# Ten gate buffers and an earlier, regrouped issue of a step's transfers in a fused window-attention and mixture-of-experts kernel

## Chip, cores and metric

The kernel runs on one core of one Trainium2 chip. The metric is the device time of one execution in microseconds (us), from the first to the last instruction and what the launch adds around them; a lower number is better. The figure for the kernel before is the median of 3 runs.

## What is computed

The input `x` is a float32 image of shape (2, 128, 256, 256): 2 images, 128 channels, 256 by 256 pixels. The layer does two things, one after the other, each with a residual addition:

```python
x = x + conv_ref(_ln_c(x), W_qkv, W_out, rel_height, rel_width)   # windowed attention
t = _to_tokens(x)                                                 # one token per pixel
t = t + ffn_ref(_ln_t(t), router_w, router_b, expert_w, expert_b) # mixture of experts
```

The first is attention in windows of 8 by 8 query pixels that look at 12 by 12 keys and values (4 heads of 32 channels, relative position terms, and a fixed mask that leaves only every second row and column of the keys). The second sends every pixel through a router with 8 experts, each a 128 by 128 matrix:

```python
router_probs = softmax(x @ router_w + router_b)
top_p, top_i = top_k(router_probs, 2)
top_p = top_p / sum(top_p)
expert_out = einsum('bnd,edc->bnec', x, expert_w) + expert_b
out = einsum('bnk,bnkc->bnc', top_p, gathered(expert_out, top_i))
```

The kernel computes all 8 experts for every pixel and weights each with a gate, which is zero for the 6 experts that were not picked.

## The kernel before

**Tiling.** The image is cut into 64 strips of 8 rows (`strips`), and the attention of a strip falls into 4 planes, by the parity of row and column, since the mask lets a query see only keys of one parity. The main loop (L809) runs over `n_planes + 7` steps, one plane of 512 queries a step, 263 steps in all. A step also works on one *pair of rows* of an older strip (512 pixels) in the mixture of experts, as a pipeline over three steps: in one step the router statistics are made (`norms`, `route`), in the next the gates are spread over all partitions, and in the one after that the products with the expert matrices finish.

**Order.** From L808 on the order of the instructions of each engine is the order of the program text: nothing is rescheduled. All DMAs of the loop are issued by SyncE (SP), one after the other, in program order. A DMA that has to wait for a semaphore holds up every DMA behind it. Completion is counted on eight semaphores that are used in turn, so each DMA also waits until the DMA eight places before it has landed.

**One step, as its engines see it.**

- *TensorE (PE)*: the score product with the keys (L474, L491), the projections `pu`, `pv`, `pk`, `pq` of the next plane (L408, L350, L423, L445), the last four expert products, for experts 4, 6, 7, 5 (L714, called at L851), the sums and the values of the attention (L512, L522), the statistics `plt` (L580), the first expert products 0, 1, 2 (L714), the output projection `po` (L550), expert product 3.
- *VectorE (DVE)*: from the end of the attention (L522) on, a long chain: `sT`, `rc`, `rT`, `o` (L532 to L542), the statistics `plg` and `rstd` (L589, L232 to L239), the residual `xt` (L555), the whole of `route` (L613 to L645), the transposed gates `gT` (L651), then `uT` (L413), which frees the PSUM buffer that `pq` (L445) needs; after that `au` (L397), `xs` (L699), the six products `xe` of pixels and gates for experts 0, 1, 2, 3, 4, 6 (L705) and the residual of the experts (`end`, L720).
- *GpSimd (POOL)*: after a copy that waits for the DVE's `xe` of expert 6 (`behind`, L709), the `xe` of expert 5, the normalised rows `xn` (`ln1`, L276, which needs the transfer `rb`), in every fourth step a copy `halo` (L250), and the `xe` of expert 7.
- *ScalarE (ACT)*: exponentials, copies out of PSUM, the squares, and one-element copies that pace DMAs (below).

**The transfers.** `spread` (L648) writes the transposed gates `gT` to a small DRAM tensor `gd` with two DMAs (L659). From there, each row is read back broadcast to all 128 partitions, 256 KB for each: `rb` (L665, for `ln1`), `sb` (`fetch_means`, L694) and eight gates `gb` (`fetch`, L680 to L689), one an expert. `fetch` first writes one element of the buffer by an engine of the caller's choice (DVE memset or ACT copy), and SP's DMA waits for that element. This sets the earliest time of the DMA in the order of that engine. Further there are `send_values` (L369, one or two DMAs of `vr` to `vrows`), `take_values` (L374 to L384, two DMAs `vwin` that read them back in window form), `load_x` (L115, the next rows of `x`), and `store` (L750).

The order of the 17 or 18 DMAs of a step on SP before the change is: `gd`, `gd`, `vrows`, `rb`, `sb`, `vwin`, `vwin`, gates 0, 1, 2, the load, gate 3, the store, gate 4, gate 6, and then, already in the next step, gates 5 and 7, which are paced by ACT copies (L831 after the router's exponential, L836 after the copy `vr`). Gate 4 is paced by ACT as well (L887, after `rstd`); gate 6 comes last in the step (L900).

**Code alignment.** At the head of each step L823 fills PE's instruction stream with NOPs, so that a block boundary of 256 instructions falls 95 instructions behind the head:

```python
BLOCK, FIRST_LIMIT = 256, 95
nc.tensor.addr_align(BLOCK, offset=BLOCK - FIRST_LIMIT)
```

The step has 768 instruction places on PE, so three boundaries. The score product of L474 takes 64 instructions (32 weight loads and 32 matmul passes), so the first boundary is 31 instructions into L491; the second, 256 later, follows the first pass of the expert product at L851; the third lies in the values' product L522.

## Time and profile before

| | us |
|---|---|
| median of 3 runs (4413.12 to 4420.50) | 4416.81 |
| the profiled execution's own time | 4415.92 |
| its span, first to last instruction | 4414.1 |
| PE busy | 4254.2 (96%) |
| DVE busy | 3844.2 (87%) |
| ACT busy | 1455.9 (33%) |
| POOL busy | 1092.5 (25%) |
| mean granted TensorE clock | 0.992 |

The largest transfers of the loop, from the page's list of DMA issues:

| transfer | count | KB each | median us to landing |
|---|---|---|---|
| gates `gb` | 2048 | 256 | 5.7 |
| `vwin` | 512 | 240 | 5.4 |
| load of `x` | 256 | 256 | 6.4 |
| store | 256 | 256 | 6.0 |
| `sb` | 256 | 256 | 4.2 |
| `rb` | 249 | 256 | 3.4 |
| `gd` | 516 | 16 | 3.3 |

"PE busy" counts the time in which matmuls are in the pipeline; its ends are modelled, so idle times of PE are best read from the starts of neighbouring matmuls. A step takes about 16.8 us. In this text, times within a step are counted from the start of its output projection `po` (L550): "+2.5" is 2.5 us after it.

### The profile page before, as it was taken

Reading aid. Unit: us, or ns where it says so; the run is one execution under the profiler, and the core shown is the slowest. Engines: PE = TensorE matmul, PEld = TensorE weight load, DVE = VectorE, ACT = ScalarE, POOL = GpSimd, SP = SyncE. Lnnn points to the kernel's source line nnn. Section 1 sums busy time; section 2 is a strip of 40 time slices with the busy share of each in tenths; the row PEclk is TensorE's granted clock in tenths of the full one; section 3 lists DMA queues with packets and bytes.
Section 4 is the critical chain, followed back from the end, with each engine's and each line's share of the span. In section 5 each row is a group of like instructions: output and inputs, shape, how many; then the busy total and the mean of one; then the engine's idle time right before and its main releaser. Section 6 shows DMA issues by size and latency. Waiting matters only on the chain. (4 is left out here: it accounts for less than half of the span.)

```text
span 4414.1 us, 224656 instructions
## 1 busy us (share of the span) xinstructions
PE 4254.2 (96%) x94273; PEld 2453.1 (56%) x94273; DVE 3844.2 (87%) x11850; ACT 1455.9 (33%) x3774; POOL 1092.5 (25%) x1126
## 2 busy tenths in 40 slices
PE   7899999999999999999999999999999999999987
PEld 4555555555555555555555555555555555555553
DVE  5788889888898988898888889988888888888877
ACT  3333333333333333333333333333333333333321
POOL 1122222222222222222222222222222222222211
PEclk9999999999999999999999999999999999999998
DMA  4677777777787777777878777777778777777865
GB/s 121 201 246 229 244 232 241 246 234 233 233 242 232 242 238 235 244 234 243 243 233 243 231 242 232 243 239 239 242 229 244 238 236 233 232 232 239 243 195 183
DMA packets 824580, 1022.19 MB, mean 232 GB/s; under 512 B 137634, under 2 KB 409634, under 8 KB 823594
## 3 DMA queue, kind: packets, MB, share of 16 engines
q1 hardware_dynamic: 822864, 1007.52, 74.6%
q8 instruction: 769, 12.60, 1.2%
q14 instruction: 217, 1.78, 0.1%
q10 hardware_dynamic: 730, 0.29, 0.0%
HBM read 863.78 MB, written 143.75 MB: 228 GB/s over the span
## 5 line engine op out<-in xcount | busy, mean ns | idle before, releaser
L714 PE MATMUL acc<-xe,ew 128*128 128x512 f32 x4096 | 1935.8, 602 | 66.7 <-issue 44.9
L714 PEld LDWEIGHTS acc<-xe,ew 128*128 128x128 f32 x4096 | 759.2, 190 | 1001.6 <-issue 931.2
L705 DVE TENSOR_TENSOR xe<-xs,gb 128x512 f32<-128x512 f32 x1536 | 951.0, 687 | 12.3 <-DMA gb<-gd 2.2
L709 POOL COPY last<-xe 128x1 f32<-128x1 f32 x256 | 47.0, 184 | 3119.1 <-DVE gb L688 3109.9
L705 POOL TENSOR_TENSOR xe<-xs,gb 128x512 f32<-128x512 f32 x512 | 650.8, 1272 | 2.5 <-PE acc L714 1.6
L276 POOL TENSOR_TENSOR xn<-xt,rb 128x512 f32<-128x512 f32 x249 | 374.0, 1502 | 171.5 <-DMA rb<-gd 165.4
L491 PE MATMUL att<-qs,kcol 32*64 32x32 f32 x32768 | 396.9, 226 | 4.8 <-issue 4.7
L491 PEld LDWEIGHTS att<-qs,kcol 32*64 32x64 f32 x32768 | 394.4, 131 | 6.3 <-issue 5.8
L522 PEld LDWEIGHTS att<-pT,vwin 64*32 64x32 f32 x32768 | 348.0, 105 | 37.5 <-issue 0.4
L522 PE MATMUL att<-pT,vwin 64*32 64x32 f32 x32768 | 343.3, 200 | 0.2 <-issue 0.2
L350 PEld LDWEIGHTS pv<-wt,xn 128*128 128x128 f32 x2048 | 270.5, 192 | 127.4 <-issue 80.1
L434 ACT COPY kcol<-pk 128x560 f32<-128x560 f32 (+2 forms) x344 | 318.9, 927 | 52.4 <-PE pk L423 49.0
L499 ACT ACTIVATE pT<-att 128x1024 f32<-128x1024 f32 x256 | 261.9, 1023 | 221.3 <-PE att L491 220.7
L532 DVE STREAM_TRANSPOSE sT<-att 128x512 f32<-128x512 f32 x256 | 183.5, 717 | 133.4 <-PE att L522 124.1
L445 PE MATMUL pq<-xn,wt 128*128 128x512 f32 x512 | 272.8, 614 | 23.4 <-DVE uT L413 21.4
L408 PE MATMUL pu<-xn,wrel 128*128 128x512 f32 x512 | 293.0, 654 | 0.0
L574 ACT ACTIVATE sq<-xt 128x512 f32<-128x512 f32 x505 | 291.8, 629 | 0.0
L397 DVE STREAM_TRANSPOSE au<-auT 128x512 f32<-128x512 f32 x256 | 272.5, 1064 | 9.0
L550 PE MATMUL po<-o,wt 128*128 128x512 f32 x512 | 265.1, 599 | 8.2 <-DVE o L542 5.8
L350 PE MATMUL pv<-wt,xn 128*128 128x128 f32 x2048 | 271.3, 275 | 0.9 <-issue 0.9
L423 PE MATMUL pk<-xn,wt 128*128 128x512 f32 (+2 forms) x528 | 263.4, 581 | 2.4 <-issue 1.3
L474 PEld LDWEIGHTS att<-au,keys 32*64 32x64 f32 x8192 | 117.2, 132 | 227.7 <-PE po L550 183.5
(2696 smaller groups left out, 4884.0 us busy)
## 6 DMA issues: line engine op xcount, KB each, us to landing
gb<-gd SPq DMA_DIRECT2D x2048, 256.0 KB, 5.7
vwin<-vrows SPq DMA_DIRECT2D x512, 240.0 KB, 5.4
xt<-in_x_dram SPq DMA_DIRECT2D x256, 256.0 KB, 6.4
sb<-gd SPq DMA_DIRECT2D x256, 256.0 KB, 4.2
out_dram<-xt SPq DMA_DIRECT2D x256, 256.0 KB, 6.0
rb<-gd SPq DMA_DIRECT2D x249, 256.0 KB, 3.4
vrows<-vr SPq DMA_DIRECT2D x168, 256.0 KB, 4.0
vrows<-vr SPq DMA_DIRECT2D x160, 128.0 KB, 3.6
```

Source lines behind the costliest of these rows:

```text
L276: eng.tensor_tensor(xn[i % 2][:, :, :, k, 1 : PC + 1], ln1_src(i, k).rearrange("p (y j x) -> p y x j", y=2, x=2), rb.rearrange("p (y j x) ...
L350: nc.tensor.matmul(pv[:, j * P : (j + 1) * P], lhsT=xp[:, k, 1 : PC + 1], rhs=wv, start=True, stop=True,)
L397: nc.vector.transpose(au.rearrange("p m a s -> p a s m"), auT[n % 2])
L408: nc.tensor.matmul(pu, lhsT=wrel, rhs=inner, start=True, stop=True)
L434: nc.scalar.copy(places[:, 1 : NP - 1], windows(new[:, :, KC - 3 :], 0, NP - 2))
L445: nc.tensor.matmul(pq, lhsT=wq, rhs=inner, start=True, stop=True)
L491: nc.tensor.matmul(sc[rows, h, 32 * t : 32 * t + 32], lhsT=kk[hp, half * HP + t, :], rhs=qs[hp, m0 : m0 + 2].rearrange("p m a s -> p (m a ...
L522: nc.tensor.matmul(av[hp, half, 32 * t : 32 * t + 32], lhsT=vv[rows, t, hp], rhs=pT[rows, h, 32 * t : 32 * t + 32], start=True, stop=True,)
L550: nc.tensor.matmul(po, lhsT=wo, rhs=state["o"].rearrange("p f z -> p (f z)"), start=True, stop=True)
L574: nc.scalar.activation(sq, src, AF.Square)
L705: eng.tensor_tensor(self.xe[e], self.xs, self.gb.pop(e), ALU.mult)
L714: nc.tensor.matmul(self.acc, lhsT=ew[:, e, :], rhs=self.xe.pop(e), start=(e == 0), stop=not self.xe)
```

## The change

- The buffers for gates go from 8 to 10.
- All eight gates of a pair of rows are fetched in the step that spreads them, and all are paced by DVE memsets; the three ACT copies of a step are gone.
- Behind `sb`, which stands where it stood, gate 0 now comes ahead of the `vwin` reads, and the two `vwin` reads are issued apart: the first after gate 0, the second after gate 3. The load comes between gates 1 and 2, the store before gate 4.
- No instruction of PE or POOL changes or moves.

The order on SP after the change: `gd`, `gd`, `vrows`, `rb`, `sb`, gate 0, `vwin`, gate 1, the load, gates 2 and 3, `vwin`, the store, gates 4, 6, 5, 7; then the next step's `gd`.

```diff
-    def take_values(n):
-        for half in range(2):
+    def take_values(n, halves=(0, 1)):
+        for half in halves:
...
-            self.gb[e] = gates.tile([P, NT * P], F32, tag="gb", name=f"gb{nm}", bufs=8)
+            self.gb[e] = gates.tile([P, NT * P], F32, tag="gb", name=f"gb{nm}", bufs=10)
...
             next(rout, None)
-            nxt.fetch(5, nc.scalar)
             for _ in rout:
                 pass
             next(score, None)
             next(ahead, None)
-            nxt.fetch(7, nc.scalar)
...
             nxt.means()
             new.fetch_means()
-            if n + 1 < n_planes:
-                take_values(n + 1)
-            for e in (0, 1, 2, 3):
+            for e in (0, 1):
                 nxt.times(e, dve)
             new.fetch(0, dve)
+            if n + 1 < n_planes:
+                take_values(n + 1, (0,))
+            for e in (2, 3):
+                nxt.times(e, dve)
+            new.fetch(1, dve)
+            load_x((n + 9) // 4, (n + 9) % 4, paced=True)
             for e in (4, 6):
                 nxt.times(e, dve)
-            new.fetch(1, dve)
+            new.fetch(2, dve)
             ex.end()
-            new.fetch(2, dve)
+            new.fetch(3, dve)
+            if n + 1 < n_planes:
+                take_values(n + 1, (1,))
+            while to_store:
+                store(*to_store.pop())
             next(attn, None)
+            new.fetch(4, dve)
             next(attn, None)
+            new.fetch(6, dve)
+            new.fetch(5, dve)
             ex = nxt
             next(norm, None)
-            load_x((n + 9) // 4, (n + 9) % 4, paced=True)
-            new.fetch(3, dve)
-            while to_store:
-                store(*to_store.pop())
             next(ahead, None)
             ex.product(0)
             made = next(norm, None)
+            new.fetch(7, dve)
             ex.product(1)
             ex.product(2)
-            new.fetch(4, nc.scalar)
...
             ex.product(3)
             next(outp, None)
-            new.fetch(6, dve)
```

## The prediction

> **What bounds the kernel now.** I read the page first: which engine is full, and how busy the DMA queues are.

> ```profile
> PE 4254.2 (96%) x94273; PEld 2453.1 (56%) x94273; DVE 3844.2 (87%) x11850; ACT 1455.9 (33%) x3774; POOL 1092.5 (25%) x1126
> ...
> q1 hardware_dynamic: 822864, 1007.52, 74.6%
> q8 instruction: 769, 12.60, 1.2%
> ```

> PE is the bound. Queue q8 moves PE's own code: 769 blocks of 16 KB, three a step. Then I took the 238 steps between 200 and 4200 us, from `po` to `po`. An undisturbed step takes 16.27 us (the value met most often); all together they lie 124 us above 238 such steps. By stretches of PE, from start to start, this splits into: expert products 4, 6, 7, 5 (L714) 66.7; `pk` to `pq` 36.8; `pq` to the first product 11.0; scores (L491) 7.2. The change can only touch these 124 us, or add to them. The waits name the second part, and who is late ahead of it:

> ```profile
> POOL xn L276 <- DMA rb<-gd: 165.4, 129, 29.2
> PEld pq L445 <- DVE uT L413: 162.9, 235, 2.2
> PE acc L714 <- issue: 44.9, 73, 2.2
> PE pq L445 <- DVE uT L413: 21.4, 48, 1.4
> ```

> (Total us, times, longest.) `pq` waits for the DVE's `uT`. The idle time at L714 has no releaser ("issue"). The timeline of one step shows it:

> ```profile
> 2007.93 1.02 PE L445 MATMUL pq<-xn,wt 128*128 128x512 f32 x2
> ...
> 2008.38 1.69 SPq L659 DMA_DIRECT2D gd<-gT  x2
> ...
> 2008.79 0.59 PE L714 MATMUL acc<-xe,ew 128*128 128x512 f32 x1
> ...
> 2010.23 3.17 PE L714 MATMUL acc<-xe,ew 128*128 128x512 f32 x7 [0.85 <-issue]
> ```

> One pass runs, then PE stands still, exactly at the block boundary. The packet records of q8 (in the trace, printed by no view) tell why: in this step a code block was fetched from 2008.04 to 2008.99, and the second pass began 1.24 us later. In 99 of the 238 steps PE stalls there, and each stall ends 1.3 to 1.4 us after such a fetch; the 16 stalls in L491 sit on the first boundary in the same way. So the 66.7 and 7.2 us are late code.

> Why is a fetch late? PE crosses the first boundary at +2.5. The fetch that must be in by the second (+7.8) begins 3.1 us after the crossing (10th to 90th percentile 2.3 to 4.0). After the second boundary it is 1.65, after the third 2.1 us. When it begins, the data in service had been issued about 0.5 us before the crossing, by the counted bytes: code queues behind the data issued ahead of it. For the first boundary that is everything up to gate 4 (issued at +1.1); gate 6 (+2.1), gate 5 (+3.1) and gate 7 (+6.5) come behind it.

> The 36.8 us come from POOL. L235 is the one DVE instruction of the chain that waits while POOL works:

> ```profile
> 1282.02 1.26 POOL L705 TENSOR_TENSOR xe<-xs,gb 128x512 f32<-128x512 f32 x1
> ...
> 1282.15 1.15 DVE L235 SCALAR_TENSOR_TENSOR u__74_23799<-u__74_23799,epsc 128x8 f32<-128x8 f32 x1
> ```

> Usually L235 takes 0.17 us; here it ends with POOL's product. Summed over the steps that is 47.8 us, from late `rb` and, every fourth step, from `halo` (L250, 0.62 us). Why is `rb` late? SP's own waits:

> ```profile
> SPq L689 <- ACT gb L686: 870.7, 518, 16.9
> SPq L665 <- DMA gd<-gT: 327.3, 241, 2.7
> ```

> `gd` is issued at +6.92 (median) although `gT` is ready at +5.65: it stands behind gate 7, whose ACT copy comes after the copy `vr`.

> **The change, part by part**, in us over the 238 steps.

> *(a) Three ACT copies become three DVE memsets, two more of them between L522 and `uT`.* A memset takes 0.06 us, yet `xe` to `xe` takes 0.61 us with one between and without. Does POOL block it, as it does L235? The timeline has one in the middle of a product of POOL (1.28 us from 2013.67):

> ```profile
> 2014.07 0.06 DVE L688 MEMSET gb<- 128x1 f32 x1
> ```

> No. Bounds 0 to 2 x 0.06 x 238 = 29, and I take +5, near the rows. The memsets' waits are on readers at least three DVE instructions or a step back; the ACT copies lay beside PE, so their end gains nothing.

> *(b) `gd` and `rb` come earlier.* Gate 7 is no longer ahead of `gd`: 1.27 us gained at the issue, so `rb` goes out at about +8.9 instead of +10.3, and POOL never waits for it. What stays is `halo`. Gain between 0 and 36.8; I take -30, and note that the stall at the next boundary then sees an earlier deadline, counted in (c).

> *(c) Code for the second boundary.* Gates 6, 5 and 7 are now issued before +2.5, so three more transfers are ahead of the fetch. Against that, the queue starts earlier. From the time the `vwin` pair is served (about +14.0) to the fetch (+5.6, or 21.9) it serves nine transfers now, 7.9 us; with 1.15 for each `vwin` that is 0.80 for each of the rest. After the change the run begins with `rb`, served from about +10.4 (issue plus 1.5), and fourteen transfers are ahead: 12 x 0.80 + 2 x 1.15 = 11.9, so the fetch begins at 22.3, which is +6.0, 0.4 later than now. With 0.72 each, the shortest service I saw in the row of gates, it is 10.9 and +5.0, 0.6 earlier. I shift the measured lateness of each step, without the `pq` waits, by s and sum what is positive: s = -0.5 gives 24, -0.25 gives 44, 0 gives 73, +0.25 gives 111, +0.5 gives 157. Today it is 66.7 + 11.0 = 78. I take s = +0.3, near the loaded rate, since the queue stays loaded: 120, so +42. Bounds -54 and +79.

> *(d) Code for the first boundary, fetched at the third (+12.4).* Now `rb` and `sb` are ahead of it. After the change SP no longer waits for `vrows` to land before it can issue a gate, and by +11.9 it has issued `rb`, `sb`, gate 0, one `vwin`, gate 1 and perhaps the load: from 10.4 on, four gate-sized services and a `vwin` end at 14.75, five at 15.55, against a start at 14.5 now. Shift between +0.2 and +1.0; the same sum over this boundary's margins gives 12 at +0.25, 30 at +0.75, 44 at +1.0, from 7 now. I take +0.75, the middle rounded up since SP then issues a DMA every 0.5 us against 0.8 of service: +23. Bounds +5 and +37.

> *(e) The rest.* `vwin`, the load and the store have most of a step until they are needed (5.4, 6.4 and 6.0 us to landing), so their new places cost nothing by themselves; if that cover were gone, L522 would wait for `vwin`. On SP, a DMA waits for the eighth before it: gate 6 for the first `vwin`, gate 5 for gate 1, gate 7 for the load. Landing takes 5 to 7 us under load, so these three may slip by about 1 us; behind them stands only `gd`, at +5.65, and they should be out by +2. Zero.

> *Sum*: +5 - 30 + 42 + 23 = +40. The profiled execution took 4415.92 (span 4414.1), so 4456; the median of the runs is 0.9 above it, hence **4457**.

> [...]

> **The rivals.** *R1, the queue drains sooner (faster).* Everything starts 1.4 us earlier and idle DMA time around +10 to +13 is filled. If the service is 0.72, s is about -0.5: (c) -54, (b) -30, (d) +5, (a) 0: -79, or 4338. For it: the gates 1 to 3 do take 0.7 to 0.8 each in the byte count; against it: 7.9 us for nine is what the whole run needs. It decides from the point where gate 7 is served before +5.3. *R2, no change.* With s = 0, (c) is 73 - 78 = -5, and 5 - 30 - 5 + 23 = -7: 4410, within 0.2% (9 us), which is about what a measurement of this kernel can tell from no change. For it: the two ends of (c) lie on both sides of it. Against it: it needs the terms to cancel. *R3, memsets blocked by POOL.* Two under POOL's work at 0.6 us each: 238 x 1.2 = 286, 4700. The row at 2014.07 speaks against it. That the change does nothing is excluded: the order on SP differs in each step.

> **How the numbers follow.** My case, code late at both boundaries, 0.62; R1 0.25; R2 0.10; R3 0.03. My case alone runs from 4430 (s = +0.25, (d) at +5) to 4528 (s = +0.5, (d) at +37, (b) only -10). R1 spreads some 35 us about 4338, so a third of it lies above 4350; I end the range there and at 4530, which leaves out about 0.17 below and a few hundredths above. Faster 0.25, within 0.2% 0.10, slower 0.65.

> **What would show it.** POOL's wait for `rb` nearly gone, L235 at 0.17 us but for every fourth step, `pq` no longer waiting for `uT`: (b). Stalls at L714 still there and as long or longer: (c). Stalls in L491 in many more than 16 steps: (d). If L714 runs without them, the queue drains sooner than I count, and R1 holds. A long memset is R3.

## The result, and the profile after

| kernel | median us | runs | ratio to before (95% interval) |
|---|---|---|---|
| before | 4418.66 | 4413.12 to 4424.38 | |
| after | 4646.06 | 4632.39 to 4658.08 | 1.0514 (1.0476 to 1.0551) |

The change makes the kernel 5.1% slower; 4457 had been forecast, in a range from 4350 to 4530. The profiled execution after took 4654.43 us (span 4652.6). The page first, engines and queues:

```profile
PE 4313.0 (93%) x94273; PEld 2510.5 (54%) x94273; DVE 3810.2 (82%) x12618; ACT 1389.8 (30%) x3006; POOL 1087.5 (23%) x1126
...
q1 hardware_dynamic: 822864, 1007.52, 75.2%
q8 instruction: 769, 12.60, 1.1%
```

PE's work is the same, its share of the span falls from 96 to 93%. The data queue q1 moves the same bytes, but 75.2% of 4652.6 us is more time in service than 74.6% of 4414.1: 3499 against 3293 us. The waits (us in total, times, longest):

```profile
PE att L491 <- issue: 167.1, 183, 3.3
...
POOL xn L276 <- DMA rb<-gd: 82.4, 17, 29.3
...
PE acc L714 <- issue: 47.1, 80, 1.6
...
PE att L522 <- issue: 40.5, 67, 1.8
...
PEld pq L445 <- DVE uT L413: 33.3, 96, 1.1
```

Two lines are as foretold: POOL waits for `rb` 17 times instead of 129, and `pq`'s wait for `uT` shrinks from 162.9 to 33.3. The first line is the loss: PE now stands 167.1 us in the scores, with no releaser. By stretches of PE between 200 and 4200 us, over the 10th percentile of each as in the prediction: L491 195.1 (7.2 before), L714 55.7 (66.7), L522 47.9 (0.8), `pu` and `pv` 36.3 (2.0), `pk` to `pq` 9.1 (36.8), `pq` to the first product 0.2 (11.0). The sum of these differences is +220 of the 239 us by which the profiled executions differ; the window holds 225 steps after and 238 before, which is why it is not all.

One step of the timeline shows the mechanism. First SP's issues (start, duration, engine, line, transfer):

```profile
1995.02 0.33 SPq L665 DMA_DIRECT2D rb<-gd  x1
1995.44 0.38 SPq L694 DMA_DIRECT2D sb<-gd  x1
1995.99 0.32 SPq L689 DMA_DIRECT2D gb<-gd  x1
1996.41 0.38 SPq L381 DMA_DIRECT2D vwin<-vrows  x1
1997.12 0.33 SPq L689 DMA_DIRECT2D gb<-gd  x1
1997.50 0.42 SPq L115 DMA_DIRECT2D xt<-in_x_dram  x1
1998.32 1.50 SPq L689 DMA_DIRECT2D gb<-gd  x2
1999.92 0.47 SPq L381 DMA_DIRECT2D vwin<-vrows  x1
```

and then PE in the same step and at the start of the next:

```profile
1998.84 1.14 PE L522 MATMUL att<-pT,vwin 64*32 64x32 f32 x105
2000.13 0.33 PE L522 MATMUL att<-pT,vwin 64*32 64x32 f32 x23 [0.15 <-issue]
...
2006.38 0.35 PE L491 MATMUL att<-qs,kcol 32*64 32x32 f32 x15
2007.79 1.04 PE L491 MATMUL att<-qs,kcol 32*64 32x32 f32 x82 [1.06 <-issue]
```

The 105th matmul of L522 is the third block boundary, crossed at 2000.0. From `rb` to the double `gb`, eight transfers of 240 or 256 KB had been issued in the five microseconds ahead of it. By the packet records of q8 the next code block was fetched from 2005.02 to 2006.33, and the scores, which stand before their 16th matmul, go on at 2007.79, 1.46 us after its end.

Over all steps the fetch begins 4.63 us after the crossing (median; 2.09 before), and the bytes issued but not yet moved at the crossing are 1168 KB against 592 KB before. In 137 steps PE stands over 0.55 us at exactly the 16th matmul of L491; the median end is 1.45 us behind a fetch. In 54 steps it stands at the 106th of L522, 1.41 us behind the fetch that goes with the second boundary.

### The profile page after: what moved, and what is told of

It is laid out like the page before. It is cut to its first block, busy times and chain, and to the rows that moved or that the text cites. A ratio compares the mean times of both kernels' runs of the same rounds, so it can differ in the third digit from the quotient of the medians.

```text
span 4652.6 us, 224766 instructions
## 1 busy us (share of the span) xinstructions
PE 4313.0 (93%) x94273; PEld 2510.5 (54%) x94273; DVE 3810.2 (82%) x12618; ACT 1389.8 (30%) x3006; POOL 1087.5 (23%) x1126
## 3 DMA queue, kind: packets, MB, share of 16 engines
q1 hardware_dynamic: 822864, 1007.52, 75.2%
q8 instruction: 769, 12.60, 1.1%
## 5 line engine op out<-in xcount | busy, mean ns | idle before, releaser
L714 PE MATMUL acc<-xe,ew 128*128 128x512 f32 x4096 | 1932.7, 601 | 65.3 <-issue 47.1
L714 PEld LDWEIGHTS acc<-xe,ew 128*128 128x128 f32 x4096 | 758.9, 190 | 998.5 <-issue 929.5
L705 DVE TENSOR_TENSOR xe<-xs,gb 128x512 f32<-128x512 f32 x1536 | 953.8, 686 | 12.4 <-PE acc L714 1.9
L705 POOL TENSOR_TENSOR xe<-xs,gb 128x512 f32<-128x512 f32 x512 | 650.6, 1272 | 0.9 <-issue 0.7
L491 PE MATMUL att<-qs,kcol 32*64 32x32 f32 x32768 | 434.5, 227 | 167.5 <-issue 167.1
L491 PEld LDWEIGHTS att<-qs,kcol 32*64 32x64 f32 x32768 | 414.1, 133 | 186.8 <-issue 185.5
L276 POOL TENSOR_TENSOR xn<-xt,rb 128x512 f32<-128x512 f32 x249 | 376.2, 1511 | 82.9 <-DMA rb<-gd 82.4
L522 PEld LDWEIGHTS att<-pT,vwin 64*32 64x32 f32 x32768 | 349.7, 105 | 84.3 <-issue 47.0
L522 PE MATMUL att<-pT,vwin 64*32 64x32 f32 x32768 | 351.6, 200 | 40.5 <-issue 40.5
L350 PEld LDWEIGHTS pv<-wt,xn 128*128 128x128 f32 x2048 | 291.1, 205 | 140.5 <-issue 90.6
L408 PE MATMUL pu<-xn,wrel 128*128 128x512 f32 x512 | 313.7, 696 | 0.0
L413 DVE STREAM_TRANSPOSE uT<-pu 128x512 f32<-128x512 f32 x256 | 179.1, 700 | 143.9 <-PE pu L408 143.0
L350 PE MATMUL pv<-wt,xn 128*128 128x128 f32 x2048 | 290.2, 288 | 0.9 <-issue 0.9
L445 PE MATMUL pq<-xn,wt 128*128 128x512 f32 x512 | 261.7, 592 | 0.3 <-DVE uT L413 0.3
```

The costliest lines, as they stand in the source:

```text
L276: eng.tensor_tensor(xn[i % 2][:, :, :, k, 1 : PC + 1], ln1_src(i, k).rearrange("p (y j x) -> p y x j", y=2, x=2), rb.rearrange("p (y j x) ...
L350: nc.tensor.matmul(pv[:, j * P : (j + 1) * P], lhsT=xp[:, k, 1 : PC + 1], rhs=wv, start=True, stop=True,)
L408: nc.tensor.matmul(pu, lhsT=wrel, rhs=inner, start=True, stop=True)
L491: nc.tensor.matmul(sc[rows, h, 32 * t : 32 * t + 32], lhsT=kk[hp, half * HP + t, :], rhs=qs[hp, m0 : m0 + 2].rearrange("p m a s -> p (m a ...
L522: nc.tensor.matmul(av[hp, half, 32 * t : 32 * t + 32], lhsT=vv[rows, t, hp], rhs=pT[rows, h, 32 * t : 32 * t + 32], start=True, stop=True,)
L705: eng.tensor_tensor(self.xe[e], self.xs, self.gb.pop(e), ALU.mult)
```

## The experiments

All were timed beside the kernel before on the same chip; the ratio carries the comparison. L491, L714 and L522 are the stretches' excess in us between 200 and 4200 us, "fetch" is the median start of the code fetch after the third crossing, "queue" is the summed time of q1's packets, divided by 16 DMA engines and 256 planes (both worked out from the packet records).

| kernel | us | ratio (95%) | L491 | L714 | L522 | fetch | queue |
|---|---|---|---|---|---|---|---|
| before | 4408 to 4426 | | 7 | 67 | 1 | 2.09 | 12.86 |
| after | 4646.06 | 1.0514 (1.0476 to 1.0551) | 195 | 56 | 48 | 4.63 | 13.67 |
| e1_load_store_back | 4601.25 | 1.0443 (1.0414 to 1.0472) | 111 | 78 | 70 | 4.24 | 13.83 |
| e2_values_together | 4462.72 | 1.0132 (1.0102 to 1.0163) | 58 | 33 | 42 | 3.86 | 12.81 |
| e3_only_gate7 | 4379.41 | 0.9934 (0.9913 to 0.9955) | 52 | 19 | 3 | 3.84 | 12.92 |
| e4_boundary_later | 4606.13 | 1.0471 (1.0427 to 1.0514) | 167 | 0 | 95 | | 13.72 |
| e5_gate7_later012 | 4352.05 | 0.9845 (0.9813 to 0.9877) | 21 | 19 | 0 | 3.07 | 12.95 |
| e6_gate7_later012_gate6 | 4336.60 | 0.9808 (0.9780 to 0.9836) | 22 | 8 | 2 | 2.95 | 12.96 |
| e7_after_gates_later | 4494.15 | 1.0169 (1.0127 to 1.0210) | 61 | 102 | 12 | 3.58 | 13.17 |
| e8_moves_only | 4710.67 | 1.0659 (1.0619 to 1.0700) | 147 | 180 | 1 | 4.27 | 14.24 |
| e9_pair_behind_gate0 | 4594.30 | 1.0391 (1.0358 to 1.0424) | 190 | 14 | 40 | 4.82 | 13.30 |
| e10_apart_only | 4339.96 | 0.9818 (0.9785 to 0.9850) | 11 | 28 | 0 | 2.66 | 13.44 |
| e11_moves_pair | 4553.31 | 1.0301 (1.0266 to 1.0335) | 111 | 93 | 2 | 4.09 | 13.66 |
| e12_pair_behind_gate1 | 4432.27 | 1.0031 (1.0012 to 1.0051) | 33 | 98 | 1 | 3.25 | 13.47 |
| f1_no_value_reads | 4370.48 | 0.9888 (0.9871 to 0.9905) | 64 | 1 | 4 | 3.93 | 11.00 |
| f2_pair_ahead_of_means | 4379.87 | 0.9914 (0.9895 to 0.9933) | 16 | 26 | 0 | 2.89 | 13.04 |
| f3_one_more | 4584.63 | 1.0379 (1.0352 to 1.0406) | 92 | 82 | 14 | 3.99 | 14.06 |

Sorted by "fetch", L491 climbs with it through 16 kernels, with a few places exchanged: 7 to 22 us up to 3.1, 33 at 3.25, 52 to 64 from 3.6 to 3.9, 92 to 111 from 4.0 to 4.25, 147 at 4.27, 190 and more beyond 4.6. (For e4 the third boundary lies elsewhere, so its start is not given.)

### Is it code? e4 and f3

e4, on the kernel after: `-BLOCK, FIRST_LIMIT = 256, 95` / `+BLOCK, FIRST_LIMIT = 256, 127`.

> The changed kernel with all block boundaries of PE's code 32 instructions later (FIRST_LIMIT 127 for 95). Theory: the stall in the scores goes with the boundary, from the 16th matmul of L491 to about the 32nd, and ends 1.3 to 1.5 us after a code fetch there too; time 4580 to 4700 us. Rival (the scores wait for an operand or a buffer): the stall stays at the 16th matmul, time as the changed kernel within 0.5%.

The stall moved. PE's timeline in e4:

```profile
1850.29 0.57 PE L491 MATMUL att<-qs,kcol 32*64 32x32 f32 x31
1851.95 1.18 PE L491 MATMUL att<-qs,kcol 32*64 32x32 f32 x97 [1.09 <-issue]
```

31 matmuls run, then PE stands; between 200 and 4200 us 120 stalls over 0.55 us lie at the 32nd matmul and none at the 16th, ending 1.45 us behind a fetch. In L522 they moved from the 106th to the 122nd. No operand is tied to those places: the scores wait for code.

f3 puts one transfer into the kernel before and moves nothing:

```
             nc.sync.dma_start(self.sb, to_all(self.gd, E))
+            more = gates.tile([P, NT * P], F32, tag="more", ..., bufs=1)
+            nc.sync.dma_start(more, to_all(self.gd, E))
```

> The kernel before with one more transfer of 256 KB, a second read of the means into a tile that nobody uses, behind sb; nothing else is moved. Theory (code queues behind data): the fetches at the third and first boundary start about 1 us later (2.1 to 3.1, and 3.1 to 4.0 us), stalls at L714 grow from 67 to 150 to 260 us and in L491 from 7 to 20 to 80 us, time 4520 to 4700 us, though the queue has 25% of its time free. Rival (the queue has room, code is taken in turn): 4415 to 4430 us.

```profile
POOL xn L276 <- DMA rb<-gd: 332.7, 221, 29.2
...
PE att L491 <- issue: 72.2, 106, 3.9
PE acc L716 <- issue: 60.8, 107, 1.9
```

One transfer that nobody waits for costs 3.8%, in a queue busy three quarters of the time (74.6% in the kernel before). (L716 is L714, two lines on.) The fetch at the third boundary starts 1.9 us later, more than the 1 us expected, and POOL's wait for `rb` doubles (165.4 us before). The stalls lie elsewhere than expected: L491 has 92 us, above its 20 to 80, and L714 only 82, below its 150 to 260.

### Which part of the change? e3, e8, and the undone parts

e3, on the kernel before: `bufs=10`, and gate 7 beside gate 5.

```
+            nxt.fetch(7, nc.scalar)
...
-            nxt.fetch(7, nc.scalar)
```

> The kernel before with ten buffers and gate 7 beside gate 5, all else in its old place. Theory: the gates of the next step keep their old places behind the third boundary, so L491 stays below 30 us of stalls; gd and rb leave 1.2 us earlier, POOL no longer waits for rb, and the queue is shorter at the first boundary: 4330 to 4390 us. Rival (an earlier gd brings so much data ahead of the third boundary that the scores stall anyway): 4430 to 4520 us.

As the theory said in time (0.9934), though L491 already shows 52 us, not under 30: `rb`, `sb`, the pair and gate 0 now stand ahead of the third crossing. e8 is the other half alone: gate 0 ahead of the values, reads apart, load and store moved; gates 4, 6, 5, 7 and the eight buffers as before. Against the kernel after:

```
+            nxt.fetch(5, nc.scalar)
...
+            nxt.fetch(7, nc.scalar)
...
-            new.fetch(4, dve)
...
-            new.fetch(6, dve)
-            new.fetch(5, dve)
...
-            new.fetch(7, dve)
...
+            new.fetch(4, nc.scalar)
...
+            new.fetch(6, dve)
```

> The kernel before with the other half of the change alone: gate 0 ahead of the values, the values' reads apart, load and store between the gates; eight buffers, gates 4, 6, 5, 7 as before, gate 7 ahead of gd. Theory: rb leaves at +10.3 as before, so only rb, sb and gate 0 are ahead at the third boundary; stalls in L491 below 40 us; 4390 to 4450 us. With e3 then neither half alone costs what the two cost together, because the lateness counts only past 3.8 us. Rival (the moves alone are what costs): 4550 us or more.

Here my theory of that moment fell: 1.0659, worse than the whole change. From e8's waits:

```profile
POOL xn L276 <- DMA rb<-gd: 278.0, 197, 29.1
...
PE acc L714 <- issue: 169.0, 179, 2.1
...
PE att L491 <- issue: 125.0, 134, 2.2
```

So the change is a gain and a larger loss: the earlier `gd` with ten buffers gives 0.7%, the moves take 6.6%. And the queue column says that the moves do more than reorder: the packets of the same bytes take 14.24 us a step instead of 12.86. Four kernels undo single moves. e1 puts the load and the store back:

```
-            load_x((n + 9) // 4, (n + 9) % 4, paced=True)
...
-            while to_store:
-                store(*to_store.pop())
...
             next(norm, None)
+            load_x((n + 9) // 4, (n + 9) % 4, paced=True)
+            while to_store:
+                store(*to_store.pop())
```

> Theory (code for the scores is late, because its block, asked for at the third boundary, waits behind the data issued just before): without the load ahead of that crossing 256 KB less are in the way, about 1.0 us at the 252 KB/us of the changed kernel, so the fetch starts 3.7 us after the crossing instead of 4.7, the stalls in the scores (L491) fall from 195 us to 40 to 90, and the time is 4500 to 4560 us. Rival (the gates alone fill the queue, the load's place is of no matter): 4620 to 4670 us, stalls in L491 above 170 us.

e2 puts both reads ahead of gate 0:

```
             new.fetch_means()
+            if n + 1 < n_planes:
+                take_values(n + 1)
...
-                take_values(n + 1, (0,))
...
-                take_values(n + 1, (1,))
```

> Theory: both reads of the values now stand ahead of gate 0, so the queue at the third boundary is as full as in the changed kernel, and the scores stall as before: 4600 to 4700 us. Rival (it is the reads taken apart, or gate 0 ahead of them, that cost): 4430 to 4500 us, stalls in L491 below 60 us.

e9 puts the second read directly behind the first, both behind gate 0, and e11 does the same to e8:

```
-                take_values(n + 1, (0,))
+                take_values(n + 1)
...
-                take_values(n + 1, (1,))
```

> The changed kernel with the second read of the values directly behind the first, so that the two go out as a pair again (still behind gate 0). New theory (a read of the values slows the transfers served next to it, and two reads apart slow twice as many): the packets of one step fall from 12.7 to about 11.8 us of queue time, stalls in L491 fall from 195 to 50 to 110 us, time 4450 to 4530 us. Rival (the place of gate 0 ahead of the values, and seven transfers issued by the crossing, are the cost): the fetch at the third boundary starts 4.6 us or later, time 4600 us or more.

> The kernel e8 (the moves alone) with the values' reads as a pair behind gate 0. New theory: the packets of one step fall from 13.3 to about 12 us of queue time and both stalls with them: 4430 to 4530 us against 4711 in e8. Rival (gate 0 ahead of the values, load and store earlier are the cost): 4620 us or more.

e1 gained 0.7%, where 1.9 to 3.1% had been expected: its fetch starts at 4.24, since gates 2 and 3 move up into the load's place. e2 went against the theory and into the rival's range. e9 and e11 then part the rival's two causes. Neither came out as the theory said: e9 saved 0.4 us in the queue instead of 0.9 and kept 190 us in L491, and e11, at 4553 us, lies between its two cases. Joining the reads is worth 1.0514 to 1.0391 in the kernel after and 1.0659 to 1.0301 in e8; taking gate 0 back behind the pair is worth another 1.0391 to 1.0132. So both cost, gate 0 ahead of the values most in the kernel after.

e7 keeps the reads apart and all gates within the step, but lets the DVE reach the memsets later (the lines in their old places, which go, are not shown):

```
             for e in (4, 6):
                 nxt.times(e, dve)
+            new.fetch(0, dve)
+            load_x((n + 9) // 4, (n + 9) % 4, paced=True)
             ex.end()
+            new.fetch(1, dve)
...
             next(attn, None)
+            new.fetch(2, dve)
+            new.fetch(3, dve)
```

> The changed kernel with gates 0 to 4 and the load each a place later on the DVE, all still within the step. Theory: by the crossing only rb, sb, one vwin and perhaps gate 0 are issued, the fetch starts 3.0 to 3.6 us after it, stalls in L491 fall from 195 to 20 to 80 us, those in L522 (40 to 70 us, from rb going out ahead of the second boundary's fetch) stay: 4450 to 4530 us. Rival (it is the ten buffers and the gates within the step as such): 4600 us or more.

As expected in time and in L491; but L522 fell to 12 and L714 rose to 102: what is issued later than the third crossing stands ahead of the first.

### A version that beats both: e5, e6, and its limits, e10, e12, f2

e5 takes e3 and puts the memsets of gates 0, 1, 2 one place later each (the second part of this diff); e6 also moves gate 6 behind the first boundary (the first and last part):

```
-            nxt.fetch(5, nc.scalar)
-            nxt.fetch(7, nc.scalar)
+            for e in (6, 5, 7):
+                nxt.fetch(e, nc.scalar)
...
-            new.fetch(0, dve)
             for e in (4, 6):
                 nxt.times(e, dve)
-            new.fetch(1, dve)
+            new.fetch(0, dve)
             ex.end()
-            new.fetch(2, dve)
+            new.fetch(1, dve)
             next(attn, None)
+            new.fetch(2, dve)
...
-            new.fetch(6, dve)
```

> As e3_only_gate7, with the memsets of gates 0, 1 and 2 one place later each (behind the products 4 and 6, behind the sum, behind the next part of the attention), so that only rb, sb and the two vwin stand ahead of the fetch at the third boundary, not gate 0 and half of gate 1 too. Theory: that fetch starts about 2.9 us after the crossing (3.84 in e3), stalls in L491 fall from 52 to below 15 us, and the time is 4325 to 4360 us. Rival (what is taken from the third boundary comes back at the first, since the same bytes follow later): the stalls at L714 grow from 19 us to 50 or more, time 4375 to 4420 us.

> As e5, with gate 6 too taken behind the first boundary (ACT copies for gates 6, 5, 7 together). Theory: one transfer less ahead of the first boundary's fetch, 0.9 us earlier; stalls at L714 below 10 us; 10 to 20 us faster than e5. Rival (gate 7 now leaves so late that gd waits in the queue and rb comes late again): POOL waits for rb in over 100 steps, slower than e5 by 10 to 40 us.

Both as the theory said in time, 0.9845 and 0.9808, though L491 keeps 21 us in e5, not under 15. SP's timeline of one step of e6 shows the difference to the kernel after:

```profile
2007.03 1.18 SPq L659 DMA_DIRECT2D gd<-gT  x2
2008.30 0.54 SPq L369 DMA_DIRECT2D vrows<-vr  x1
2010.77 0.33 SPq L665 DMA_DIRECT2D rb<-gd  x1
2011.18 0.68 SPq L694 DMA_DIRECT2D sb<-gd  x1
2011.97 0.90 SPq L381 DMA_DIRECT2D vwin<-vrows  x2
2013.42 2.04 SPq L689 DMA_DIRECT2D gb<-gd  x3
2015.51 0.42 SPq L115 DMA_DIRECT2D xt<-in_x_dram  x1
2016.61 0.32 SPq L689 DMA_DIRECT2D gb<-gd  x1
```

The pair follows `sb` at once and no gate goes out ahead of it. What is left of stalls: L491 22, L714 8, `pk` 14.

Three kernels move the reads of the values within e6. e10 puts the second one behind gate 1:

```
-                take_values(n + 1)
+                take_values(n + 1, (0,))
...
             new.fetch(1, dve)
+            if n + 1 < n_planes:
+                take_values(n + 1, (1,))
```

> The kernel e6 with only the second read of the values moved behind gates 0 and 1. New theory: gates 0 to 2 and sb take 0.2 to 0.4 us more each in the queue, 0.6 to 1.0 us more a step in all; the first boundary's fetch comes later, stalls at L714 grow from 8 to 25 to 70 us: 4355 to 4420 us. Rival (the reads apart cost nothing by themselves; one transfer less ahead of the third boundary even helps): 4325 to 4345 us.

e12 puts the pair there, and f2 puts it ahead of `new.fetch_means()`:

```
-                take_values(n + 1)
...
             new.fetch(1, dve)
+            if n + 1 < n_planes:
+                take_values(n + 1)
```

> The kernel e6 with the pair of reads of the values behind gate 1 instead of ahead of gate 0. Theory: by the third crossing only rb, sb and perhaps gate 0 are issued; the fetch starts 1.5 to 2.3 us after it (2.95 in e6), stalls in L491 fall from 22 to below 8 us, L714 as in e6: 4315 to 4335 us. Rival (the pair served later pushes what follows over the first boundary): stalls at L714 of 30 us or more, 4345 to 4380 us.

> The kernel e6 with the pair of reads of the values ahead of sb, the read of the means. If what is slow is the stretch from +11 to +16, the pair (1.0 to 1.2 us each in every kernel) takes that stretch and sb is served in 0.95 us or less: packets of 12.7 us or less a step, stalls in L491 below 22 us, time 4320 to 4340 us. If the slowness belongs to the read of the means itself, sb stays at 1.2 us or more, and the time is 4335 to 4370 us.

e10 took half a microsecond more in the queue (13.44; 0.6 to 1.0 more had been expected) and lost nothing, as its rival said: L714 rose by 20 us, and L491, with one read less ahead of it, fell by 11. e12 was a miss: the fetch came later (3.25), not earlier, the queue took 13.47, L714 grew to 98, and the time, 4432 us, was worse than the rival's too. f2 met neither case: `sb` still took 1.2 us, and the time was worse than both. The order `rb`, `sb`, pair, gates is the best that I found.

### Why is the queue slower? f1, open

f1, on the kernel after, leaves out the reads of the values from the ninth plane on:

```
-            if n + 1 < n_planes:
+            if n + 1 < 8:
                 take_values(n + 1, (0,))
...
-            if n + 1 < n_planes:
+            if n + 1 < 8:
                 take_values(n + 1, (1,))
```

> The changed kernel without the two reads of the values from the ninth plane on (the attention then works on old values), so that two transfers a step are gone. Theory of late code: the fetch at the third boundary starts below 3.8 us after the crossing in nearly all steps, stalls in L491 fall below 30 us, time 4320 to 4420 us. On the open point: if it is the reads of the values that slow their neighbours, sb and gate 0 take 0.7 to 1.1 us each in the queue; if transfers served from +11 to +16 of a step are slow whatever stands next to them, sb and gate 0 still take 1.2 us or more each.

The time came as expected; the fetch (3.93, not below 3.8) and L491 (64 us, not below 30) did not. `sb` and gate 0 still take 1.51 and 1.45 us in the queue, by the counted bytes, with no read of the values near them. So the reads are not what slows them. Over the kernels, `sb` takes 1.1 to 1.3 us where the pair or one read follows it (before, e2, e3, e5, e6, e7, e10), and 1.3 to 1.8 where another read of `gd` follows it directly (after, e1, e8, e9, e11, e12, f1, f3); that next read takes 1.2 to 1.45, gates 2 and 3 between 0.65 and 1.05. f2 fits neither, with the pair ahead of `sb` and gate 0 behind it. One stretch of the step does not explain it: the slow services begin at +11.5 in f1 and at +14.7 in f3. Its cause stays open.

## Why the prediction was wrong

**(a) Memsets.** Right. Undisturbed (10th percentile), the DVE's chain from `sT` to the start of `uT` takes 8.98 us before and after; +5 had been allowed. Where `uT` starts later after the change, it waits for PE's `pu`.

**(b) Earlier `gd` and `rb`.** Right: -28 us of the stretch `pk` to `pq` against -30. L235's excess fell from 47.8 to 1.6 us. e3 shows this part by itself, with 6 us left in that stretch. Not all of the fall in `pq`'s own wait is this part's: e3, with 10 waits for `rb`, keeps 91.4 of the 162.9 us; that the kernel after has only 33.3 is likely because PE itself comes late to `pq`.

**(c) Code for the second boundary.** The sum is wrong by its sign within its bounds: -22 us (L714 and `pq`) against +42. The fetch starts 3.27 us after the first crossing, 0.14 later than before, so the shift of +0.3 was near. But counted from where PE goes on behind the boundary, it starts at 2.9, against 3.1 before: where PE has just stood in L491, the queue has had time to drain (about 840 KB are issued and not yet moved at that point in the steps with a stall over 1.5 us, about 1260 KB in those with none). The steps of the kernel after bear this out. In the 32 with no stall in L491 the fetch starts 3.3 us after PE goes on, and L714 loses 0.42 us on average; in the 43 with a stall over 1.5 us it is 2.8 us and 0.10. In e8, which has much at both places, the steps part the same way (0.90 and 0.32 us). Whether this is the whole of the fall stays open.

**(d) Code for the first boundary: the step that failed.** "Five at 15.55, against a start at 14.5", a shift of at most +1.0, worth 37 us. Measured from the third crossing, the fetch starts at 4.63 us instead of 2.09, a shift of +2.5, and the stalls in L491 grew by 188. Two terms of the sum were too small. The service: I took 0.80 us a gate, the mean of a whole run of transfers, but `rb`, `sb`, gate 0, `vwin` and gate 1 are the first of the run, and they took 1.17, 1.41, 1.33, 1.05 and 1.03: 5.99 us instead of 4.35. The trace of before showed it: the counted bytes give `rb` 1.13 and `sb` 1.23 there and 0.7 only from gate 2 on. And the count: PE, held up by its stalls, comes to the crossing at a median of +13.3 and not at +12.4, and by then SP has issued the load (+12.1), which I had called perhaps, and gate 2 (+12.7), which the sum left out; `rb` is served from 10.74, not 10.4. The curve over the margins, on the other hand, was too steep: at shifts of 0.6 to 1.0 (e10, f2, e6, e5) there were 11 to 22 us of stalls, where it gives about 24 to 44. Carried on with the trace of before, it gives some 250 us at +2.5, against 195.

**(e) The rest at zero.** Wrong. The prediction asked of `vwin`, the load and the store only when they are needed themselves. They cost by what they push and by the order they leave: undone, they are worth 0.7% (e1, load and store) to 3.8% (e2, the values' reads). And the third boundary's own need was left out: the 47.9 us in L522 are late code too, of the fetch that goes with the second boundary. Counted from the first pass of the product at L851, the last one ahead of the boundary, `rb` is now issued at a median of 0.4 us, 2.8 before; e3 has 1.2 and 3 us of stalls. In 52 of the 54 steps of the kernel after that stall there, `rb` had gone out ahead of the second pass, and the fetch starts 2.95 us behind that pass, about when `rb` has been served (0.1 us after it, median); in the other steps it starts 0.8 us behind. So `rb` stands ahead of the code there. An early `rb` is not enough by itself: 103 of the 170 other steps have `rb` out ahead of the second pass too, and f1, with `rb` as early and a shorter queue, has only 4 us.

**A term nobody had.** `pu` and `pv` lost 34 us, see below. Against the sum, (d) lost 165 us more, L522 47 and these two 34, while (c) gave back 64. That last part was luck: no term of the sum had it.

**The rivals.** R1's mechanism, a queue that drains sooner at the first boundary, was there in e3, e5 and e6 (L714 19, 19 and 8 us), but the rest of the change spoils it; R3 was rightly excluded. In the kernel after, 195 + 56 + 48 us are late code (L491, L714, L522).

## What to carry to other kernels

A transfer has two prices: when it is needed, and what it stands ahead of. In this long unrolled kernel the engine's own code, fetched by DMA, waited behind the data issued ahead of it (the fetch began 2.09 us after the third crossing with 592 KB outstanding, 4.63 us with 1168 KB), so price each moved transfer at every block boundary it now precedes, with the service times of that place in the run and not with the mean. And take a regrouping apart before judging it: here one part of it (gate 7 no longer ahead of `gd`, and ten buffers) was worth 0.7% and, with the gates paced to go out behind the crossings, 1.9%, while the rest cost ten times its gain.

## What was not expected of the hardware

About half of the long stalls are paid twice. PE around one stall of the kernel after, and the profile's windows there (us, busy times of PE, PE's weight loads, DVE, ACT and POOL, granted clock of PE, DMA share, GB/s):

```profile
2076.37 0.35 PE L491 MATMUL att<-qs,kcol 32*64 32x32 f32 x15
2078.33 1.36 PE L491 MATMUL att<-qs,kcol 32*64 32x32 f32 x113 [1.61 <-issue]
2079.62 2.08 PE L408 MATMUL pu<-xn,wrel 128*128 128x512 f32 x2
2081.49 1.80 PE L350 MATMUL pv<-wt,xn 128*128 128x128 f32 x8
```

```profile
2076.50:2078.30 1.80, 0.22 (x23) 0.12 (x11) 1.67 (x6) 0.23 (x1) 0.00 (x0) 1.00 1.11 242
2078.30:2079.40 1.10, 1.07 (x108) 1.07 (x109) 0.91 (x6) 0.00 (x0) 0.00 (x0) 1.00 1.05 337
2079.40:2080.60 1.20, 1.20 (x28) 0.68 (x15) 0.24 (x1) 0.87 (x1) 0.00 (x0) 0.60 1.03 393
2080.60:2082.00 1.40, 1.40 (x5) 0.85 (x4) 0.27 (x1) 0.15 (x1) 0.00 (x0) 0.50 0.75 258
```

And the time of the packets depends on their order: those of the same 1007.52 MB take between 12.81 and 14.24 us a step on the 16 engines (e2, e8). Why is open.
